# Delta u stored in 32-row half units, and the step size finished in its PSUM bank

## The chip, the cores and the metric

The kernel runs on one core of a Trainium2 chip. The metric is the device time of one launch in microseconds (us). The engines of the core are named as in the profile: PE (TensorE, matrix products), PEld (its weight loads), DVE (VectorE), ACT (ScalarE), POOL (GpSimd) and SP (SyncE, which here only issues transfers). A name with a q, such as SPq or ACTq, is an instruction by which a queue issues a transfer. Each engine takes its instructions in a fixed order.

## The reference, cut to what matters

The program is a network of four layers on 4 images of 96 channels and 64 x 64 pixels (4096 positions). Layer 0 is a selective state-space scan over four directions, layer 1 a deformable convolution with gathers, layer 2 a Fourier mixer with a feed-forward part, layer 3 a linear attention with a feed-forward part. The change touches layer 0 alone. Its core, for each of 4 images and 4 directions, with 192 channels and 16 states per channel:

```python
delta = jax.nn.softplus(dts + delta_bias[None, :, :, None])
...
def step(h, inp):
    d_t, u_t, b_t, c_t = inp
    dA = jnp.exp(d_t[..., None] * A)
    h = dA * h + (d_t * u_t)[..., None] * b_t[:, :, None, :]
    y = jnp.einsum('bkdn,bkn->bkd', h, c_t)
    return (h, y)
h0 = jnp.zeros(u.shape[:3] + (A.shape[-1],), u.dtype)
_, ys = lax.scan(step, h0, (dl, ul, bl, cl))
```

So there is a step size delta (softplus of a projection) per channel and position, a product delta times u, a decay exp(delta A) per channel and state, and the recurrence along the 4096 positions.

## The kernel before, in words

**The scan.** A unit is 8 channels by 16 states, which fill the 128 partitions, over 1024 positions. There are 4 images x 4 directions x 4 stretches of positions x 24 groups of 8 channels, 1536 units. A block is the 64 channels of one stretch, 8 units: `i` from 0 to 3 and `q` from 0 to 1. For each unit:

- `fetch` (L907, L911) has ACT's queue load the step sizes of 8 channels, each repeated for 16 states, into `da`, five units ahead. `fetch_block` (L926) has SP's queue load delta u for a block in two transfers, six units ahead. `fetch_step` (L918) loads B and C for a stretch.
- `decay` (L932): ACT takes the exponential of `da`.
- `inflow` (L938): two PE matmuls spread delta u over the 128 partitions into `db`, a PSUM tile of two banks with two buffers. Delta u is kept as three bf16 pieces whose sum is the fp32 value, so the 96 rows of the operand are 3 pieces x 32 channels, and the 0/1 matrix `rep` picks the unit's 8 channels and adds the pieces.
- `enter` (L952): DVE multiplies `db` by B in place. `recur` (L960): DVE scans.
- `weigh` (L967, L969): POOL saves the last state and multiplies by C. `total` (L983, L988): PE sums over the states into `py`. `settle` (L999) copies it out on ACT, `store` (L1006) writes it on SP's queue.

**The step sizes.** `before(b)` prepares image b: normalisation, convolution, projections, and then `steps`, one chain for each of 8 chunks of 512 positions and 6 groups of rows (4 of 128 channels of one direction, 2 of 64 channels of two directions): 192 chains. A chain is: PE projects into a PSUM bank `pd` (L769); ACT makes abs, exp, ln(1 + e) into `lw` and 1 + e into `w1` (L771 to L775); DVE corrects `w1` (L778); POOL corrects `lw` (L780); DVE adds max(pd, 0) into `rl` (L782), the step size; DVE multiplies it by u into `ex` (L785 where u is read transposed, L791 otherwise); SP stores `rl` (L794). Then ACT and PE split `ex` into the three bf16 pieces `du` (L798 to L808), and SP stores those (L812). `lw` and `w1` have one buffer, `rl` and `du` two, `ex` three.

**The order of the work.** The scan's units are laid down in order, and between them a planner lays down steps of two other streams: `ends` (the preparation of images 0 to 3, then layers 2 and 3 of each image) and `middle` (the output part of layer 0, `behind`, and layer 1, in series for each image). Each step states its cost on each engine, the PSUM banks that it holds (three are shared by these streams), and the buffers that it takes and frees. The planner keeps a clock for each engine and lays down a step where that leaves room. The program's order on each engine is the order of laying down. A step can only begin if its first engine would not idle for it, so a step that starts on ACT is laid down when ACT's planned end has passed the step's ready time. What is not laid down when the last unit is reached follows after the scan, alone.

**Waits.** An instruction waits for semaphores. The tile framework adds these waits by itself[...]. [...]

Of the kernel before, what the change touches and what calls it, by code (L numbers as in the profile page):

```python
# [10 lines left out]
BF16 = mybir.dt.bfloat16  # L11
# [9 lines left out]
L = H * W  # L21
# [23 lines left out]
def prepare(x, **w):  # L45
# [51 lines left out]
    dtp[64 : 64 + R + 1, 2:] = dtw[2:].transpose(2, 0, 1)  # L97
    a["dtw"] = dtp

    al = w["L0_conv_A_logs"].reshape(KG, DI // D8, D8, NS)  # L100
    a["al"] = c(al.transpose(3, 2, 0, 1).reshape(128, KG * DI // D8))

    ds = w["L0_conv_Ds"].reshape(KG, NG, 64).transpose(2, 1, 0)
    a["ds"] = c(np.concatenate([ds, ds]))
# [22 lines left out]
    for n in (2, 3):  # L127
# [14 lines left out]
    a["cen_c"] = wide(cen[128:], 256)  # L142

    p = np.arange(128)
    rep = (p[:, None, None] % 32 == 8 * np.arange(4)[None, :, None] + p[None, None] % 8).astype(f)
    a["rep"] = c(rep)
    a["fold"] = c(
        (p[:, None, None] % 8 + 8 * np.arange(4)[None, :, None] == np.arange(32)[None, None]).astype(f)
    )
    yy, xx = np.divmod(np.arange(L).reshape(32, 128).T, W)  # L150
    ki, kj = np.divmod(np.arange(9), 3)
# [368 lines left out]
class Unit:  # L520


    def __init__(self, b, k, step, g, i, q):
        self.b, self.k, self.step, self.g, self.i = b, k, step, g, i
        self.s = i + 4 * q
        self.back = k >= 2
        self.j = NT - 1 - step if self.back else step
        self.n = 8 * g + self.s
        self.key = f"{b}_{k}_{self.j}_{g}_{self.s}"
        self.first_of_block = i == 0 and q == 0  # L530
        self.first_of_step = self.first_of_block and g == 0
        self.ts = slice(self.j * T, (self.j + 1) * T)
        self.bc = self.du = None
# [5 lines left out]
class Layer0:  # L539
# [7 lines left out]
    def __init__(self, ctx, net, x1):  # L547
        self.net, self.x1 = net, x1
        tc, nc, ins = net.tc, net.nc, net.ins
        wp = ctx.enter_context(tc.tile_pool(name="l0w", bufs=1))  # L550
        for name in ("fold", "al", "ds"):
            setattr(self, name, net.load(name, wp))

        nc.scalar.activation(self.al, self.al, AF.Exp)
        nc.vector.tensor_scalar_mul(self.al, self.al, -1.0)

        dsum = wp.tile([128, NG], F32, name="dsum")
        nc.vector.reduce_sum(dsum, self.ds, axis=mybir.AxisListType.X)
        self.skip = wp.tile([128, NG, 128], F32, name="skip")
        for g in range(NG):  # L560
            nc.vector.tensor_scalar_mul(self.skip[:, g, :], net.ident, dsum[:, g : g + 1])

        self.wc_d = net.dram.tile([C, 9, 256], F32, name="wc_d")
        self.rep = wp.tile([128, 4, 128], BF16, name="rep16")
        self.minus = wp.tile([128, 128], BF16, name="minus")
        nc.vector.tensor_scalar_mul(self.minus, net.ident, -1.0)
        with tc.tile_pool(name="l0prep", bufs=1) as tp:
            nc.vector.tensor_copy(self.rep, net.load("rep", tp))
            w_in = net.load("w_in", tp)
            cw = tp.tile([C, 9, 256], F32, name="cwr")  # L570
            nc.sync.dma_start(cw, ins["cw"].partition_broadcast(C))
            nc.vector.tensor_mul(cw, cw, w_in[:, :256].unsqueeze(1).to_broadcast([C, 9, 256]))
            nc.sync.dma_start(self.wc_d, cw)
        dram = net.dram
        self.u_d = [dram.tile([DI, L], F32, name=f"u{b}") for b in range(B)]
        self.z_d = [dram.tile([DI, L], F32, name=f"z{b}") for b in range(B)]
        self.de_d = [dram.tile([KG, DI, L], F32, name=f"de{b}") for b in range(B)]
        self.du_d = [dram.tile([KG, 3, DI, L], BF16, name=f"du{b}") for b in range(B)]
        self.bc_d = [dram.tile([KG, 2 * NS, L], F32, name=f"bcd{b}") for b in range(B)]
        self.y_d = [dram.tile([KG, DI, L], F32, name=f"y{b}") for b in range(B)]  # L580
        self.sp = ctx.enter_context(tc.tile_pool(name="l0s", bufs=2))
        self.banks = ctx.enter_context(ExitStack())
        self.ps = self.banks.enter_context(tc.tile_pool(name="l0q", bufs=1, space=PSUM))


        self.ready, self.summed = set(), set()

        self.scanned = (0.0, 0.0)

        self.settled = 0.0  # L590
# [160 lines left out]
    def steps(self, b, ks, j, us, dtw, sm, xdbl):  # L751

        net = self.net
        nc = net.nc
        cs = slice(j * CH, (j + 1) * CH)
        tk = f"{b}_{j}_" + "".join(str(k) for k in ks)
        both = len(ks) == 2

        def tile_of(name, bufs):
            return sm.tile([128, CH], F32, name=f"{name}{tk}", tag=name, bufs=bufs)  # L760

        yield wait(new=True, takes="ex lw")


        pd = net.mm(f"pd{tk}")
        for k in ks:
            q = k % 2
            o, m = (pd[64 * q : 64 * q + 64], slice(128, DI)) if both else (pd, slice(0, 128))
            nc.tensor.matmul(o, lhsT=dtw[:, k, m], rhs=xdbl[q, j], start=True, stop=True)  # L769
        ex = tile_of("ex", 3)  # L770
        nc.scalar.activation(ex, pd, AF.Abs)  # L771
        nc.scalar.activation(ex, ex, AF.Exp, scale=-1.0)
        lw, w1 = tile_of("lw", 1), tile_of("w1", 1)
        nc.scalar.activation(lw, ex, AF.Ln, bias=net.one)
        nc.scalar.activation(w1, ex, AF.Identity, bias=net.one)  # L775
        yield cost(pe=2.2 if both else 1.1, act=2.7, holds=1, takes="rl")
        rl = tile_of("rl", 2)
        nc.vector.scalar_tensor_tensor(w1, w1, -1.0, ex, ALU.add, ALU.subtract)  # L778
        yield cost(dve=0.7, holds=1)
        nc.gpsimd.tensor_sub(lw, lw, w1)  # L780
        yield cost(pool=1.3, holds=1)
        nc.vector.scalar_tensor_tensor(rl, pd, 0.0, lw, ALU.max, ALU.add)  # L782
        yield cost(dve=0.7, frees="lw")
        if not both and ks[0] % 2:
            nc.vector.tensor_mul(  # L785
                ex.rearrange("p (w h) -> p w h", h=H),
                rl.rearrange("p (w h) -> p w h", h=H),
                us[1][:, j * NR : (j + 1) * NR, :],
            )
        else:  # L790
            nc.vector.tensor_mul(ex, rl, us[2 if both else 0][:, cs])  # L791
        parts = ((0, 64, ks[0], 128), (64, 128, ks[1], 128)) if both else ((0, 128, ks[0], 0),)
        for p0, p1, k, c0 in parts:
            nc.sync.dma_start(self.de_d[b][k][c0 : c0 + p1 - p0, cs], rl[p0:p1])  # L794
        yield cost(dve=0.7, takes="du", frees="rl")

        du = sm.tile([128, 3, CH], BF16, name=f"du{tk}", tag="du", bufs=2)
        nc.scalar.copy(du[:, 0, :], ex)  # L798
        yield cost(act=0.6, new=True)
        pr = net.mm(f"pr{tk}")  # L800
        nc.tensor.matmul(pr, lhsT=net.ident, rhs=ex, start=True, stop=False)  # L801
        nc.tensor.matmul(pr, lhsT=self.minus, rhs=du[:, 0, :], start=False, stop=True)
        nc.scalar.copy(du[:, 1, :], pr)
        yield cost(pe=1.5, act=0.6, holds=1, frees="ex")
        nc.tensor.matmul(
            pr, lhsT=self.minus, rhs=du[:, 1, :], start=False, stop=True, skip_group_check=True
        )
        nc.scalar.copy(du[:, 2, :], pr)  # L808
        yield cost(pe=0.4, act=0.6)
        for p0, p1, k, c0 in parts:  # L810
            dst = self.du_d[b][k][:, c0 : c0 + p1 - p0, cs]
            nc.sync.dma_start(dst.rearrange("s c t -> c s t"), du[p0:p1])  # L812
        self.ready.update((b, k, both, j) for k in ks)
        yield wait(frees="du")

# [66 lines left out]
    def fetch(self, u, before):  # L882
# [24 lines left out]
                nc.scalar.dma_start(add[64 * h : 64 * h + 64], src[c0 : c0 + 64, halves[h]])  # L907
        self.net.clock.add(ACT, 0.6, self.scanned[1])
        u.da = sp.tile([128, T], F32, name=f"da{u.key}", tag="da", bufs=6)
        src = self.de_d[b][k][c0 + D8 * u.s : c0 + D8 * u.s + D8, ts]  # L910
        nc.scalar.dma_start(u.da, src.unsqueeze(0).to_broadcast([NS, D8, T]))  # L911

    def fetch_step(self, u):
# [5 lines left out]

    def fetch_block(self, u):  # L920

        u.du = []
        for q in range(2):
            t = self.sp.tile([96, T], BF16, name=f"du{u.key}_{q}", tag=f"du{q}")
            c0 = 64 * u.g + 32 * q
            self.net.nc.sync.dma_start(t, self.du_d[u.b][u.k][:, c0 : c0 + 32, u.ts])  # L926
            u.du.append(t)

    def decay(self, u):
        u.decayed = self.net.clock.add(ACT, 1.15, 0.0)  # L930
# [1 line left out]
        self.net.nc.scalar.activation(u.da, u.da, AF.Exp, scale=self.al[:, a : a + 1])  # L932

    def inflow(self, u):
        u.spread = self.net.clock.add(PE, 0.8, self.scanned[1])
        db = self.ps.tile([128, 2, CH], F32, name=f"db{u.key}", tag="db", bufs=2)
        for h in range(2):
            self.net.nc.tensor.matmul(  # L938
                db[:, h, :],
                lhsT=self.rep[:96, u.s % 4, :],  # L940
                rhs=u.du[u.s // 4][:, h * CH : (h + 1) * CH],
                start=True,
                stop=True,
            )
# [847 lines left out]
```

## Time and profile before

| what | value |
|---|---|
| median of 3 runs | 8837.66 us (8813.62 to 8846.13) |
| profiled execution, its own time | 8879.74 us |
| its span | 8877.9 us |
| DVE busy | 6807.1 us (77%) |
| PE busy | 6652.4 us (75%) |
| POOL busy | 5620.9 us (63%) |
| ACT busy | 4943.6 us (56%) |
| granted TensorE clock, mean | 0.805 |

A line of a group reads: line of the kernel, engine, operation, result<-operands by the program's names, shapes, count | busy time in us, mean time of one in ns | idle time of the engine just before these, and what ended most of it. A line of a wait reads: who <- for what: us in total, times, longest. In a timeline: start, duration, engine, line, operation, and in brackets the idle time ahead of it and what ended it. The 40 digits of a row of section 2 are busy tenths of 40 equal slices of the span.

### The profile page before, as it was taken

What the parts mean: (1) busy time and instruction counts of PE and PEld (TensorE: products, weight loads), DVE (VectorE), ACT (ScalarE), POOL (GpSimd) and SP (SyncE); (2) the same over time, 40 slices, a digit from 0 to 9 for tenths busy, and PEclk for the clock granted to TensorE, in tenths of its full rate; (3) what the DMA queues carried; (4) which work ended last, traced back from release to release, by engine and by line L of the source; (5) the groups of instructions that cost most, each with busy time, mean ns of one, the idle gap of its engine ahead of it and who ended that gap; (6) DMA issues with size and microseconds to landing.
All of it is one profiled execution on the core that took longest, in us unless ns stands there. A gap on an engine that the chain in (4) does not pass through costs nothing.

```text
span 8877.9 us, 96298 instructions
## 1 busy us (share of the span) xinstructions
PE 6652.4 (75%) x31960; PEld 2922.8 (33%) x31960; DVE 6807.1 (77%) x5091; ACT 4943.6 (56%) x9062; POOL 5620.9 (63%) x4307
## 2 busy tenths in 40 slices
PE   6665967687767778777667888776778877787797
PEld 2111311122122224311222455222445532265383
DVE  0488889987888988788898887788878888636514
ACT  3564656555556768745566666445656774423323
POOL 0365656665668888666588888566887886447400
PEclk8786977788778779877777888787888887788797
DMA  1476777767678888876788988676888987444310
GB/s 48 134 201 178 187 186 223 202 176 184 190 204 228 234 225 231 212 181 187 200 226 223 230 223 225 152 181 173 212 228 211 234 204 170 108 128 146 96 55 11
DMA packets 775989, 1608.40 MB, mean 181 GB/s; under 512 B 247809, under 2 KB 339357, under 8 KB 773382
## 3 DMA queue, kind: packets, MB, share of 16 engines
q10 hardware_dynamic: 244224, 843.17, 37.0%
q1 hardware_dynamic: 457542, 532.51, 22.2%
q0 software_dynamic: 73728, 226.57, 9.7%
q8 instruction: 256, 4.19, 0.2%
q14 instruction: 239, 1.96, 0.1%
HBM read 1345.62 MB, written 256.29 MB: 180 GB/s over the span
## 4 chain that ended last, share of the span: by engine, by line
PE 35%; DVE 28%; DMA 16%; ACT 8%; issue 8%; POOL 3%; SPq 2%; ACTq 1%; DVEq 0%; another core or an unknown queue 0%; POOLq 0%
DVE hh L960 14%; DVE db L952 7%; DMA du<-du 6%; PE pc L691 4%; PE py L988 4%; PE f L1428 3%; PE db L938 3%; PE ps L1334 3%; DMA da<-de 2%; ACT g L1313 2%; PE pd L1350 2%; POOL hh L969 1%; ACT da L932 1%; PE h L1469 1%; PE py L983 1%
## 5 line engine op out<-in xcount | busy, mean ns | idle before, releaser
L969 POOL TENSOR_TENSOR hh<-hh,bc 128x1024 f32<-128x1024 f32 x1536 | 3659.8, 2385 | 346.0 <-DVE hh L960 233.6
L960 DVE TENSOR_TENSOR_SCAN hh<-da,st,db 128x1024 f32<-128x1024 f32 x1152 | 2701.0, 2345 | 236.2 <-PE py L988 98.9
L952 DVE TENSOR_TENSOR db<-db,bc 128x1024 f32<-128x1024 f32 x1536 | 1863.3, 1213 | 557.5 <-PE db L938 551.6
L932 ACT ACTIVATE da<-da,w_al 128x1024 f32<-128x1024 f32 x1536 | 1741.8, 1146 | 648.2 <-DMA da<-de 295.3
L938 PE MATMUL db<-du,rep 96*128 96x512 bf16 x3072 | 1105.0, 448 | 810.8 <-DVE hh L960 748.9
L1301 POOL DMA_INDIRECT g<-table,idx x1152 | 1210.6, 1051 | 407.2 <-issue 176.0
L988 PE MATMUL py<-hh,w_fold 128*32 128x512 f32 x6144 | 1055.6, 762 | 26.6 <-POOL hh L969 8.8
L1313 ACT ACTIVATE g<-g,wt 128x96 f32<-128x96 f32 x3456 | 963.9, 364 | 167.6 <-DMA du<-du 52.2
L960 DVE TENSOR_TENSOR_SCAN hh<-da,db 128x1024 f32<-128x1024 f32 x384 | 877.1, 2284 | 68.9 <-PE py L988 22.8
L938 PEld LDWEIGHTS <-rep 96*128 96x128 bf16 x3072 | 284.5, 107 | 1764.0 <-issue 1126.3
L1334 PE MATMUL ps<-w_ident,g 128*96 128x128 f32 x3744 | 675.3, 320 | 215.0 <-ACT g L1313 138.0
L780 POOL TENSOR_TENSOR lw<-lw,w 128x512 f32<-128x512 f32 x192 | 244.2, 1272 | 825.5 <-DVE w L778 815.6
L967 POOL COPY st<-hh 128x1 f32<-128x1 f32 x1152 | 232.4, 202 | 725.3 <-DVE hh L960 682.0
L1334 PEld LDWEIGHTS ps<-w_ident,g 128*96 128x96 f32 x3744 | 480.1, 141 | 569.4 <-ACT g L1313 249.6
L691 PE MATMUL pc<-pad,wc 96*128 96x512 f32 x1152 | 547.8, 615 | 53.4 <-DMA wc<-wc_d 46.3
L1342 ACT COPY st<-ps 96x384 f32<-96x384 f32 x384 | 179.7, 472 | 458.2 <-PE ps L1334 350.6
L801 PE MATMUL pr<-ex,w_ident 128*128 128x512 f32 x384 | 281.0, 822 | 170.0 <-DVE ex L791 87.7
L778 DVE SCALAR_TENSOR_TENSOR w<-w,ex 128x512 f32<-128x512 f32 x192 | 155.1, 808 | 289.8 <-ACT w L775 289.7
L691 PEld LDWEIGHTS pc<-pad,wc 96*128 96x128 f32 x1152 | 216.5, 195 | 336.4 <-issue 305.1
L988 PEld LDWEIGHTS py<-hh,w_fold 128*32 128x32 f32 x6144 | 155.1, 123 | 516.8 <-issue 393.8
L769 PE MATMUL pd<-xd,w_dtw 103*64 103x512 f32 (+1 forms) x512 | 268.0, 802 | 65.8 <-DVE rl L782 26.1
L1350 PE MATMUL pd<-st,wdc 96*128 96x256 f32 x1152 | 302.4, 411 | 7.8 <-ACT st L1342 4.1
(250 smaller groups left out, 8807.7 us busy)
## 6 DMA issues: line engine op xcount, KB each, us to landing
da<-de ACTq DMA_DIRECT2D x1536, 512.0 KB
du<-du SPq DMA_DIRECT2D x512, 192.0 KB
bc<-bcd SPq DMA_DIRECT2D x128, 512.0 KB
du<-du SPq DMA_DIRECT2D x128, 384.0 KB
y<-yb SPq DMA_DIRECT2D x384, 128.0 KB
de<-rl SPq DMA_DIRECT2D x128, 256.0 KB
m<-in_dft SPq DMA_DIRECT2D x128, 256.0 KB
ad<-y ACTq DMA_DIRECT2D x192, 128.0 KB
```

The lines of the kernel that those rows point to most:

```text
L691: nc.tensor.matmul(pp, lhsT=wc[:, q, g * 128 : (g + 1) * 128], rhs=pad[:, r0 + dy : r0 + dy + NR, dx : dx + W], start=(q == 0), stop=(q == 8),
L801: nc.tensor.matmul(pr, lhsT=net.ident, rhs=ex, start=True, stop=False)
L932: self.net.nc.scalar.activation(u.da, u.da, AF.Exp, scale=self.al[:, a : a + 1])
L938: self.net.nc.tensor.matmul(db[:, h, :], lhsT=self.rep[:96, u.s % 4, :], rhs=u.du[u.s // 4][:, h * CH : (h + 1) * CH], start=True, stop=True,)
L952: self.net.nc.vector.tensor_mul(u.db, u.db, u.bc[:, 0, :])
L960: nc.vector.tensor_tensor_scan(u.along(u.hh), u.along(u.da), u.along(u.db), first, ALU.mult, ALU.add)
L969: self.net.nc.gpsimd.tensor_mul(u.hh, u.hh, u.bc[:, 1, :])
L988: nc.tensor.matmul(py[p0 : p0 + 32], lhsT=self.fold[:, u.i, :], rhs=hc[:, h * CH : (h + 1) * CH], start=u.sums["add"] is None and u.i == 0 ...
L1301: nc.gpsimd.indirect_dma_start(out=g[:, k, :], out_offset=None, in_=self.tables[b % 2], in_offset=bass.IndirectOffsetOnAxis(ap=idx[:, n : ...
L1313: nc.scalar.activation(pixel, pixel, AF.Identity, scale=wt[:, n, c : c + 1])
L1334: nc.tensor.matmul(pt[:, k, :], lhsT=g[:, k, c * C : (c + 1) * C], rhs=net.ident, is_transpose=True, start=(c == 0), stop=(c == corners - 1),)
L1350: nc.tensor.matmul(po, lhsT=wdc[:, k, :], rhs=st[:, k, :], start=(k == 0), stop=(k == 8))
```

## The change

Two things change in layer 0.

The first concerns the step size. DVE no longer writes it to `rl` in SBUF but back into its PSUM bank `pd`. ACT then copies `pd` to `rl`, from where it is stored, and DVE multiplies `pd` by u. `pd` is held for one step more, and `rl` is taken later.

The second concerns delta u. In DRAM it is laid out in blocks of 32 channels and 512 positions, each with its 96 rows (3 pieces x 32 channels) together, so a chain stores it in four transfers of 32 partitions, and a block is fetched in four transfers of 24 partitions with four rows each: channel 4p + i of a 32-group sits in partition p, place i. One tile holds two halves of positions (h) and two groups of 32 channels (q) at partitions 64q + 32h. The spread matmul of half h then contracts 24 rows at that partition in place of 96, as a tile of 32 rows of the array, and `rep` is one 128 x 128 matrix. A unit now takes channels i, i + 4, i + 8, ... of its 32, so `al`, `fold` and the rows of the `da` load follow. The cost that `inflow` states to the planner goes from 0.8 to 0.5.

```diff
-    rep = (p[:, None, None] % 32 == 8 * np.arange(4)[None, :, None] + p[None, None] % 8).astype(f)
-    a["rep"] = c(rep)
+    a["rep"] = c((p[:, None] % 8 == p[None] % 8).astype(f))
...
-        self.du_d = [dram.tile([KG, 3, DI, L], BF16, name=f"du{b}") for b in range(B)]
+        self.du_d = [dram.tile([KG, NCH, DI // 32, 3 * 32, CH], BF16, name=f"du{b}") for b in range(B)]
...
         yield cost(pe=2.2 if both else 1.1, act=2.7, holds=1, takes="rl")
-        rl = tile_of("rl", 2)
...
-        nc.vector.scalar_tensor_tensor(rl, pd, 0.0, lw, ALU.max, ALU.add)
-        yield cost(dve=0.7, frees="lw")
+        nc.vector.scalar_tensor_tensor(pd, pd, 0.0, lw, ALU.max, ALU.add)
+        yield cost(dve=0.7, holds=1, frees="lw")
+        rl = tile_of("rl", 2)
+        nc.scalar.copy(rl, pd)
...
-            nc.vector.tensor_mul(ex, rl, us[2 if both else 0][:, cs])
+            nc.vector.tensor_mul(ex, pd, us[2 if both else 0][:, cs])
+        yield cost(dve=0.7, act=0.6)
         parts = ((0, 64, ks[0], 128), (64, 128, ks[1], 128)) if both else ((0, 128, ks[0], 0),)
         for p0, p1, k, c0 in parts:
             nc.sync.dma_start(self.de_d[b][k][c0 : c0 + p1 - p0, cs], rl[p0:p1])
-        yield cost(dve=0.7, takes="du", frees="rl")
+        yield wait(takes="du", frees="rl")
...
         for p0, p1, k, c0 in parts:
-            dst = self.du_d[b][k][:, c0 : c0 + p1 - p0, cs]
-            nc.sync.dma_start(dst.rearrange("s c t -> c s t"), du[p0:p1])
+            for p in range(p0, p1, 32):
+                dst = self.du_d[b][k, j, (c0 + p - p0) // 32].rearrange("(s c) t -> c s t", s=3)
+                nc.sync.dma_start(dst, du[p : p + 32])
...
-        src = self.de_d[b][k][c0 + D8 * u.s : c0 + D8 * u.s + D8, ts]
+        src = self.de_d[b][k][c0 + 32 * u.q + u.i : c0 + 32 * u.q + 32 : 4, ts]
...
-        u.du = []
+        u.du = self.sp.tile([128, 4, CH], BF16, name=f"du{u.key}", tag="du")
         for q in range(2):
-            t = self.sp.tile([96, T], BF16, name=f"du{u.key}_{q}", tag=f"du{q}")
-            c0 = 64 * u.g + 32 * q
-            self.net.nc.sync.dma_start(t, self.du_d[u.b][u.k][:, c0 : c0 + 32, u.ts])
-            u.du.append(t)
+            for h in range(2):
+                p0 = 64 * q + 32 * h
+                src = self.du_d[u.b][u.k, 2 * u.j + h, 2 * u.g + q]
+                self.net.nc.sync.dma_start(u.du[p0 : p0 + 24], src.rearrange("(p i) t -> p i t", i=4))
...
-        u.spread = self.net.clock.add(PE, 0.8, self.scanned[1])
+        u.spread = self.net.clock.add(PE, 0.5, self.scanned[1])
...
-                lhsT=self.rep[:96, u.s % 4, :],
-                rhs=u.du[u.s // 4][:, h * CH : (h + 1) * CH],
+                lhsT=self.rep[64 * u.q + 32 * h : 64 * u.q + 32 * h + 24],
+                rhs=u.du[64 * u.q + 32 * h : 64 * u.q + 32 * h + 24, u.i, :],
```

More of the change, by code (lines that the diff above doesn't have):

```diff
@@ L98, in prepare @@
     a["dtw"] = dtp
-    al = w["L0_conv_A_logs"].reshape(KG, DI // D8, D8, NS)
-    a["al"] = c(al.transpose(3, 2, 0, 1).reshape(128, KG * DI // D8))
+    al = w["L0_conv_A_logs"].reshape(KG, DI // 32, D8, 4, NS)
+    a["al"] = c(al.transpose(4, 2, 0, 1, 3).reshape(128, KG * DI // D8))
     ds = w["L0_conv_Ds"].reshape(KG, NG, 64).transpose(2, 1, 0)
@@ L144, in prepare @@
     p = np.arange(128)
-    rep = (p[:, None, None] % 32 == 8 * np.arange(4)[None, :, None] + p[None, None] % 8).astype(f)
-    a["rep"] = c(rep)
+    a["rep"] = c((p[:, None] % 8 == p[None] % 8).astype(f))
     a["fold"] = c(
-        (p[:, None, None] % 8 + 8 * np.arange(4)[None, :, None] == np.arange(32)[None, None]).astype(f)
+        (4 * (p[:, None, None] % 8) + np.arange(4)[None, :, None] == np.arange(32)[None, None]).astype(f)
     )
@@ L524, in __init__ @@
         self.b, self.k, self.step, self.g, self.i = b, k, step, g, i
+        self.q = q
         self.s = i + 4 * q
@@ L563, in __init__ @@
         self.wc_d = net.dram.tile([C, 9, 256], F32, name="wc_d")
-        self.rep = wp.tile([128, 4, 128], BF16, name="rep16")
+        self.rep = wp.tile([128, 128], BF16, name="rep16")
         self.minus = wp.tile([128, 128], BF16, name="minus")
@@ L786, in steps @@
                 ex.rearrange("p (w h) -> p w h", h=H),
-                rl.rearrange("p (w h) -> p w h", h=H),
+                pd.rearrange("p (w h) -> p w h", h=H),
                 us[1][:, j * NR : (j + 1) * NR, :],
```

## The prediction

> **What bounds the kernel now.** I first read the page: span, and the sliced rows of section 2.
>
> ```profile
> span 8877.9 us, 96298 instructions
> ...
> DVE  0488889987888988788898887788878888636514
> ```
>
> VectorE (DVE) is full from the second to the 34th slice and thin after: the scan, then a tail. Next come three windows cut at the first scan (359) and the last (7670).
>
> ```profile
> 0.00:359.00 359.00, 216.86 (x452) 84.52 (x453) 39.87 (x70) 155.83 (x193) 14.83 (x19) 0.81 0.23 67
> 359.00:7670.00 7311.00, 5487.97 (x24592) 2183.32 (x24591) 6242.09 (x4241) 4441.81 (x8179) 5229.06 (x3975) 0.80 0.78 202
> 7670.00:8878.00 1208.00, 947.58 (x6916) 655.00 (x6916) 525.14 (x782) 345.92 (x690) 377.03 (x313) 0.82 0.31 87
> ```
>
> The columns are PE, PE weight load, DVE, ACT and POOL busy. In the scan, DVE works 6242 of 7311 us, PE 75%, ACT 61%, so what DVE saves or waits there counts nearly whole. The groups by shape say what it does, and the waits of that window what it waits for.
>
> ```profile
> L960 DVE TENSOR_TENSOR_SCAN hh<-da,st,db 128x1024 f32<-128x1024 f32 x1152 | 2701.0, 2345 | 236.2 <-PE py L988 98.9 <-ACT da L932 19.9 <-DVE db L952 4.6
> L952 DVE TENSOR_TENSOR db<-db,bc 128x1024 f32<-128x1024 f32 x1536 | 1863.3, 1213 | 557.5 <-PE db L938 551.6 <-PE lnc L471 2.2 <-DMA da<-de 1.5
> L774 ACT ACTIVATE lw<-ex,one 128x512 f32<-128x512 f32 x192 | 138.6, 722 | 93.7 <-DVE rl L782 84.2 <-DVE db L952 1.2 <-ACT ex L772 0.4
> ```
>
> ```profile
> DVE db L952 <- PE db L938: 551.6, 230, 20.3
> DVE hh L960 <- PE py L988: 121.7, 89, 14.8
> DVE w L778 <- ACT w L775: 50.8, 48, 6.4
> ```
>
> A unit costs 2.33 + 1.21 us on DVE, and its largest wait (230 times) is for the spread matmuls of L938. ACT's L774 already waits for DVE's L782: it writes `lw`, which has one buffer and which L782 reads. That line matters below. Then the durations (min/median/max) of the multiply by u:
>
> ```profile
> L785 DVE TENSOR_TENSOR ex<-rl,xa x60: 1027/1076/8809, 401.2 to 4667.6; 128x512 f32<-128x512 f32 x60
> ...
> L791 DVE TENSOR_TENSOR ex<-rl,xa x62: 676/692/5358, 373.6 to 4755.8; 128x512 f32<-128x512 f32 x62
> L791 DVE TENSOR_TENSOR ex<-rl,xc x61: 677/692/3519, 364.3 to 4689.7; 128x512 f32<-128x512 f32 x61
> ```
>
> The maxima are far above the medians; the page's means are 1724 (L785), 1176 and 1010 ns (L791). Last, a timeline around a long ACT stall, and two groups of the tail.
>
> ```profile
> 5183.76 1.58 SPq L926 DMA_DIRECT2D du<-du  x2
> ...
> 5212.75 0.52 ACTq L911 DMA_DIRECT2D da<-de  x1
> 5213.32 0.91 ACT L1313 ACTIVATE g<-g,wt 128x96 f32<-128x96 f32 x3 [10.90 <-DMA du<-du]
> ```
>
> ```profile
> L1107 DVE TENSOR_TENSOR xr<-po,xr x8: 660/661/689, 7432.4 to 7739.8; 96x512 f32<-96x512 f32 x8
> ...
> L1320 DVE TENSOR_TENSOR g<-g,wt x96: 1332/1351/1360, 7866.5 to 8364.1; 128x1152 f32<-128x1152 f32 x96
> ```
>
> ACT stands 10.9 us because its da load can't be issued before a du load that SP issued 28 us earlier has landed. In the built program SP's and ACT's transfers take eight completion semaphores in turn, and each waits for the one eight before it.
>
> [...] L785 and L791 read two, L952 reads one and stays within 1195 to 1292 ns. [...] no run here shows row tiles yet.
>
> **Part 1: step size in PSUM.** L782 now writes into its bank `pd`; ACT copies it to `rl` (new L786), and DVE multiplies `pd` by u. In the built order all 192 multiplies wait for exactly that copy, and in 159 places the multiply is DVE's next instruction after L782's. So DVE stands until ACT's in-order queue reaches the copy. Between the two the emission order puts ACT work of the *next* chain: in 126 of 192 places the Ln into `lw`, which by the wait above can't start before L782 ends. Queued behind it: L775's w1 (706 ns), in 76 of the 126 the last cast of `du` (L808, 576), then the copy (an equal PSUM copy, L999: 572). With 0.06 us for each change of engine (L803 to L805):
> - 71 adjacent, with Ln and cast: 0.72 + 0.71 + 0.58 + 0.57 + 0.12 = 2.7 us, 192 us
> - 35 adjacent, with Ln: 2.1 us, 74 us
> - 34 adjacent, copy alone: 0.7 us, 24 us; 19 with the cast: 1.0 us, 19 us
> - 33 with DVE work between: 0.5 us (estimate), 17 us
>
> That is 326 us. While DVE stands, PE catches up, and some of the 0.36 us per unit lost to L938 vanishes with it: about 40. I take **+290** (ends: 192 x 0.7 = 130 if ACT always runs ahead of its Ln; 500 if the cast's matmul is late too). All who wait for scans (POOL's 234 us, PE's 749) wait longer by it.
>
> The multiply then has one SBUF input and should keep its median: 64 x (1.72 - 1.06) + 128 x (1.09 - 0.69) = **-94** (0 to -100). 192 copies load ACT by 110 us; it idles 2870 us in the scan, so 0. `pd` keeps its bank for one more step, of three.
>
> **Part 2: 32-row groups.** A pair of L938 took 0.59 us (timeline at 3001.57) with one at 0.38: the second adds 0.21; at the low clock (634 ns) about 0.43. If both row tiles run at once, that is saved each unit, of a wait that is often PE stuck behind other streams. 230 waits x 0.32 = 74, and some 50 of backlog: **-120** ([...] -350 if two thirds of 551 go).
>
> Transfers: bytes are equal, but SP issues 4 instead of 1 or 2 per write and 4 instead of 2 per fetch: 512 + 384 = 896 more beside 4376. Eight semaphores then last 2.3 units instead of 2.6 between a da load and its predecessor; those within one unit rise from 378 to 499 of 1536. ACT waits some 0.2 ms for du transfers now. Say 120 more short blocks of 2 us on ACT, a third reaching DVE: **+80** (0 to 250). `rl` is freed by the same transfers; L782 waited 5.7 us for them, now the copy does. Strided da rows are as large as before: 0. [...] at 96 KB a piece I count nothing.
>
> **Part 3: what the planner moves.** With other costs and a bank held longer, side work falls back. In the built order, before: all of image 2's gathers and 6 of the last image's 8 output chunks stand ahead of the last scan. After: 45 gathers (15 groups) and all 8 chunks stand behind it, in one stream in series, and the last layers follow. Alone the tail does 96 groups in 498 us (7866.5 to 8364.1), 15 take 78; a pair of chunks takes 37 us from its POOL add (7703) to 7740, with its load about 40, three more pairs 120. Of these 198 I take **+190** (80 to 280). The scan is relieved of about 40 us of DVE work: **-40**. Head: five multiplies at 2 us, **+10**.
>
> **Sum.** 290 - 94 - 120 + 80 + 190 - 40 + 10 = +316 us. The profiled execution took 8879.74 us (span 8877.9 plus 1.8), so 9196; it stands 42 us above the median of the runs, 8837.66, to which I add: 9154, taken as 9150.
>
> **Rivals.** *Near balance*: stalls fall where DVE would have waited for PE anyway, +130, and the tail's extra costs 80: 130 - 94 - 120 + 40 + 80 - 40 = 0 to +60, 8840 to 8900. For it: 551 us of waits to hide in. Against: the Ln's place behind L782 is fixed. *PE packing wins (faster)*: L938's pair is what is late; if row tiles take 350 of the 551 us, the stall stays at 130 to 200 and the tail at 100, then about -130: 8700. It decides once the saving exceeds 440 with my other terms, or 250 with the low ones. Against: the longest waits (20.3 us) are no matmul's length. *Semaphores bite*: each burst of four write and four fetch transfers uses up all eight, and ACT, PE and DVE stall together as at 5202: +250 instead of 80 and late copies: 9400 to 9500. *The change doesn't do what it says*: row tiles run one after another; loses the 120, 9270.
>
> **Chances.** Main, with serial row tiles: 0.62, own range 8980 to 9330. Near balance 0.16, faster 0.10, semaphores 0.12. To leave out no more than 2 in 10 the range goes to 8860 and 9430. A change of 0.5% (44 us) is about what a measurement can tell: faster 0.10, within 0.07 (half of near balance), slower 0.83.
>
> **What would show it.** Right: the multiply waits for ACT's new copy, some 200 to 400 us in the scan; its mean falls to near 0.69 and 1.06; L938's pair near 0.4 us; DVE's wait for it near 430; scan window near 7430, tail near 1400. Wrong if that wait is under 150 us, if waits for `db` fall below 250, or if the tail stays at 1208.

## The result, and the profile after

The changed kernel takes 9117.26 us (median of 4 runs, 9112.59 to 9118.69) against 8841.9 us for the kernel before in the same comparison: ratio 1.0321, 95% interval 1.0298 to 1.0345. The forecast was 9150. Chips differ a little (the kernel before took 8826 to 8895 us beside the experiments), so kernels are compared below by their ratios to the kernel before; 0.01 of it is 88.4 us.

The page of the changed kernel, its span and DVE's row of slices:

```profile
span 9110.6 us, 96986 instructions
...
DVE  0478976797768887866789899888889999327613
```

The first third was nearly all 8 and 9 and now has 6 and 7 among them: it is where the step sizes of the images are made. The windows cut at the first and last scan (columns as before: PE, PEld, DVE, ACT and POOL busy, clock, DMA share, GB/s):

```profile
0.00:355.00 355.00, 219.00 (x453) 84.35 (x454) 39.79 (x70) 160.46 (x202) 14.11 (x19) 0.80 0.23 67
355.00:7740.00 7385.00, 5341.94 (x24198) 2076.64 (x24196) 6090.99 (x4208) 4432.81 (x8072) 5099.38 (x3899) 0.76 0.78 198
7740.00:9111.00 1371.00, 1068.29 (x7166) 713.22 (x7166) 593.67 (x885) 390.28 (x773) 463.54 (x384) 0.80 0.34 92
```

The scan took 74 us longer although DVE has 151 us less to do in it; the tail took 163 us longer and holds 103 more DVE instructions and 71 more on POOL. The granted clock in the scan fell from 0.80 to 0.76, which no step of the forecast had. DVE's waits in the scan window:

```profile
DVE db L957 <- PE db L943: 377.5, 183, 17.7
DVE ex L794 <- ACT rl L786: 344.7, 110, 7.8
DVE ex L788 <- ACT rl L786: 154.6, 53, 17.9
DVE hh L965 <- PE py L993: 86.1, 81, 6.2
```

Two rows are new: the multiply waits for the copy, 163 times in the scan, 499 us. The wait for `db` fell by 174. The groups by shape (busy us, mean ns, idle us ahead and what ended it):

```profile
L965 DVE TENSOR_TENSOR_SCAN hh<-da,st,db 128x1024 f32<-128x1024 f32 x1152 | 2701.3, 2345 | 195.7 <-PE py L993 67.4 <-POOL ya L1057 8.3 <-ACT da L937 8.2
L957 DVE TENSOR_TENSOR db<-db,bc 128x1024 f32<-128x1024 f32 x1536 | 1861.6, 1212 | 379.1 <-PE db L943 377.5
```

A scan and its multiply take what they took. The multiply by u, by its line's durations (min/median/max):

```profile
L788 DVE TENSOR_TENSOR ex<-pd,xa x64: 996/1031/1073, 281.9 to 4384.3; 128x512 f32<-128x512 f32 x64
```

Its maximum is now 4% above its median; before it was eight times the median (8809 against 1076). A timeline of one wait of the usual length (start, duration, engine, line, in brackets the idle time ahead):

```profile
1369.62 0.68 DVE L783 SCALAR_TENSOR_TENSOR pd<-pd,lw 128x512 f32<-128x512 f32 x1
...
1370.07 0.60 ACT L773 ACTIVATE ex<-pd 128x512 f32<-128x512 f32 x1 [1.12 <-PE pd L771]
...
1370.70 0.63 ACT L774 ACTIVATE ex<-ex 128x512 f32<-128x512 f32 x1
...
1371.37 0.72 ACT L776 ACTIVATE lw<-ex,one 128x512 f32<-128x512 f32 x1
...
1371.99 0.71 ACT L777 ACTIVATE w<-ex,one 128x512 f32<-128x512 f32 x1
1372.60 0.56 ACT L812 CAST du<-pr 128x512 bf16<-128x512 f32 x1
1373.07 0.59 ACT L786 COPY rl<-pd 128x512 f32<-128x512 f32 x1
...
1373.69 0.69 DVE L794 TENSOR_TENSOR ex<-pd,xc 128x512 f32<-128x512 f32 x1 [3.39 <-ACT rl L786]
```

DVE's L783 is done at 1370.30. ACT has just started the next chain, late because PE was; its four activations and a cast stand ahead of the copy, and DVE stands 3.39 us. In the tail, the multiply by the gather weights:

```profile
L1325 DVE TENSOR_TENSOR g<-g,wt x112: 1337/1357/1430, 7745.5 to 8631.7; 128x1152 f32<-128x1152 f32 x112
```

112 of these instead of 96: 16 groups of image 2 now stand behind the last scan. Last, PE's groups of the spread matmuls and of the sums over the states, in the kernel before and in the changed one:

```profile
L938 PE MATMUL db<-du,rep 96*128 96x512 bf16 x3072 | 1105.0, 448 | 810.8 <-DVE hh L960 748.9 <-DMA du<-du 39.2 <-ACT g L1313 7.1
L988 PE MATMUL py<-hh,w_fold 128*32 128x512 f32 x6144 | 1055.6, 762 | 26.6 <-POOL hh L969 8.8 <-ACT yb L999 8.8 <-issue 6.4
```

```profile
L943 PE MATMUL db<-du,rep 24*128 24x512 bf16 x3072 | 710.3, 462 | 1070.9 <-DVE hh L965 1043.8
...
L993 PE MATMUL py<-hh,w_fold 128*32 128x512 f32 x6144 | 1113.9, 801 | 43.6 <-ACT yb L1004 20.6
```

Busy time counts overlap once: 710.3 / 1536 is 0.46 us per pair, where the kernel before had 1105.0 / 1536 = 0.72. So two row tiles do overlap. But a matmul of `py`, which the change doesn't touch, went from 762 to 801 ns.

### The profile page after: what moved, and what is told of

It is laid out like the page before. It is cut to its first block, busy times and chain, and to the rows that moved or that the text cites. A ratio compares the mean times of both kernels' runs of the same rounds, so it can differ in the third digit from the quotient of the medians.

```text
span 9110.6 us, 96986 instructions
## 1 busy us (share of the span) xinstructions
PE 6629.2 (73%) x31816; PEld 2874.2 (32%) x31816; DVE 6724.4 (74%) x5161; ACT 4983.6 (55%) x9046; POOL 5577.0 (61%) x4301
## 4 chain that ended last, share of the span: by engine, by line
PE 19%; DVE 14%; DMA 6%; issue 4%; ACT 4%; POOL 2%; SPq 1%; ACTq 1%; DVEq 0%; POOLq 0%
DVE hh L965 7%; DVE db L957 4%; PE f L1433 3%; PE ps L1339 2%; PE py L993 2%; DMA da<-de 2%; PE pd L1355 2%; ACT g L1318 2%; POOL hh L974 1%; PE db L943 1%; PE h L1474 1%; PE yp L1513 1%; PE zp L1499 1%; ACT da L937 1%; PE py L988 1%
## 5 line engine op out<-in xcount | busy, mean ns | idle before, releaser
L974 POOL TENSOR_TENSOR hh<-hh,bc 128x1024 f32<-128x1024 f32 x1536 | 3635.4, 2369 | 349.1 <-DVE hh L965 229.8
L943 PE MATMUL db<-du,rep 24*128 24x512 bf16 x3072 | 710.3, 462 | 1070.9 <-DVE hh L965 1043.8
L993 PE MATMUL py<-hh,w_fold 128*32 128x512 f32 x6144 | 1113.9, 801 | 43.6 <-ACT yb L1004 20.6
L1318 ACT ACTIVATE g<-g,wt 128x96 f32<-128x96 f32 x3264 | 909.9, 364 | 165.3 <-DVE hh L965 57.0
L943 PEld LDWEIGHTS <-rep 24*128 24x128 bf16 x3072 | 159.7, 93 | 2127.6 <-issue 1331.8
L805 PE MATMUL pr<-ex,w_ident 128*128 128x512 f32 x384 | 331.2, 958 | 307.0 <-DVE ex L794 148.5
L771 PE MATMUL pd<-xd,w_dtw 103*64 103x512 f32 (+1 forms) x512 | 311.1, 915 | 48.5 <-DMA w_dtw<-in_dtw 19.1
L1355 PE MATMUL pd<-st,wdc 96*128 96x256 f32 x1152 | 323.9, 433 | 5.4 <-ACT du L812 3.0
L1442 ACT COPY d<-f 128x512 f32<-128x512 f32 x192 | 112.1, 584 | 362.7 <-PE f L1433 362.2
```

The lines of the kernel that those rows point to most:

```text
L943: self.net.nc.tensor.matmul(db[:, h, :], lhsT=self.rep[64 * u.q + 32 * h : 64 * u.q + 32 * h + 24], rhs=u.du[64 * u.q + 32 * h : 64 * u.q ...
L974: self.net.nc.gpsimd.tensor_mul(u.hh, u.hh, u.bc[:, 1, :])
L993: nc.tensor.matmul(py[p0 : p0 + 32], lhsT=self.fold[:, u.i, :], rhs=hc[:, h * CH : (h + 1) * CH], start=u.sums["add"] is None and u.i == 0 ...
L1318: nc.scalar.activation(pixel, pixel, AF.Identity, scale=wt[:, n, c : c + 1])
L1355: nc.tensor.matmul(po, lhsT=wdc[:, k, :], rhs=st[:, k, :], start=(k == 0), stop=(k == 8))
```

## The experiments

The theory at the start was that of the forecast: the wait for the copy and what the planner moves cost the time, row tiles win some back. Twelve kernels take the change apart. All ratios are to the kernel before:

| kernel | groups | step size in PSUM | price of the spread | ratio (95%) | scan / tail, us | clock |
|---|---|---|---|---|---|---|
| before | no | no | 0.8 | 1 | 7310 / 1208 | 0.805 |
| changed | yes | yes | 0.5 | 1.0321 (1.0298 to 1.0345) | 7384 / 1371 | 0.765 |
| e1 | yes | no | 0.5 | 0.9942 (0.9929 to 0.9954) | 7317 / 1115 | 0.776 |
| e2 | no | yes | 0.8 | 1.0314 (1.0268 to 1.0360) | 7425 / 1275 | 0.803 |
| e3 | yes | multiply first | 0.5 | 1.0212 (1.0167 to 1.0257) | 7275 / 1371 | 0.763 |
| e4 | yes | multiply first, copy a step | 0.5 | 0.9936 (0.9915 to 0.9958) | 7215 / 1211 | 0.776 |
| e5 | no | no | 0.5 | 1.0053 (1.0032 to 1.0073) | 7418 / 1110 | 0.812 |
| e6 | transfers only | no | 0.8 | 1.0061 (1.0042 to 1.0080) | 7368 / 1185 | 0.803 |
| e7 | yes | yes, two `lw` | 0.5 | 1.0258 (1.0228 to 1.0289) | 7367 / 1354 | 0.762 |
| e8 | yes | yes | 0.8 | 1.0175 (1.0142 to 1.0207) | 7372 / 1301 | 0.763 |
| e9 | yes | no | 0.8 | 0.9851 (0.9821 to 0.9882) | 7171 / 1247 | 0.776 |
| e10 | yes | multiply first, copy a step | 0.8 | 0.9908 (0.9879 to 0.9937) | 7134 / 1305 | 0.779 |
| e11 | no | multiply first, copy a step | 0.8 | 1.0065 (1.0033 to 1.0096) | 7249 / 1324 | 0.808 |
| e12 | yes, no row tiles | no | 0.8 | 0.9775 (0.9739 to 0.9811) | 7119 / 1229 | 0.814 |

"Scan" is from the first scan to the end of the last, "tail" what follows, and the clock is the mean of the span, all in the profiled execution. The price is what `inflow` tells the planner.

### The two halves apart

e1 has the groups with the price of 0.5, and the step size as before:

```diff
+        rl = tile_of("rl", 2)
...
-        nc.vector.scalar_tensor_tensor(pd, pd, 0.0, lw, ALU.max, ALU.add)
-        yield cost(dve=0.7, holds=1, frees="lw")
-        rl = tile_of("rl", 2)
-        nc.scalar.copy(rl, pd)
+        nc.vector.scalar_tensor_tensor(rl, pd, 0.0, lw, ALU.max, ALU.add)
+        yield cost(dve=0.7, frees="lw")
...
-            nc.vector.tensor_mul(ex, pd, us[2 if both else 0][:, cs])
-        yield cost(dve=0.7, act=0.6)
+            nc.vector.tensor_mul(ex, rl, us[2 if both else 0][:, cs])
...
```

> The 32-row groups alone; the step size is made in SBUF as before. Copy theory (the time is lost where VectorE waits for ScalarE's copy, and in the tail): no copy, no such wait; the spread pair falls to about 0.46 us, VectorE's wait for it from 552 to about 400 us, the tail stays near 1200 us: 8700 us (8640 to 8780). Transfer theory (896 more transfers and their semaphores make the loss): slower than before, 8900 us or more, with more ScalarE idle time that ends on a transfer than 701 us.

e2 has the step size in PSUM alone, units and price as before (the diff of the change's first part, nothing else).

> The step size in PSUM alone; delta u and the planner's cost as before. Copy theory: about 500 us of VectorE waits for the copy, 94 us back from the multiply, some 60 us of other waits hidden, a tail longer by about 130 us (all 8 output chunks of the last image stand behind the scan, no gathers of image 2): 9280 us (9180 to 9350), slower than the whole change. Transfer theory: the copy is hidden in waits for PE, 8900 us or less.

e1 came out at 8773.22 us and e2 at 9083.83 (before: 8826.06). The signs are as expected: the step size costs, with 492 us of waits for the copy in its scan, and the groups gain. e1 lies in its range; e2 lies some 100 us below its own (9180 to 9350), although the waits are of the length expected. And e1's wait for `db` did not fall (558 us), its scan took as long as before, and the whole gain sat in a shorter tail. It looked as if the planner's price had won it and the matmuls nothing. The part about the price fell with e5; the part about the matmuls is taken up in e12.

### The multiply ahead of the copy

e3 swaps the two readers of `pd` in the changed kernel, so that the multiply doesn't wait for ACT. e4 also makes the copy a step of its own for the planner:

```diff
-        rl = tile_of("rl", 2)
-        nc.scalar.copy(rl, pd)
...
             nc.vector.tensor_mul(ex, pd, us[2 if both else 0][:, cs])
+        yield cost(dve=0.7, holds=1)
+        rl = tile_of("rl", 2)
+        nc.scalar.copy(rl, pd)
-        yield cost(dve=0.7, act=0.6)
+        yield cost(act=0.6)
```

That is e4. In e3 the first added line is absent and the last pair is as in the changed kernel.

> The whole change with two statements exchanged: VectorE's multiply is laid down before ScalarE's copy, all else in the same order. Copy theory: the multiply no longer waits, ScalarE waits for the multiply in its place; about 500 us of VectorE waits go, some 50 to 100 come back because ScalarE is held up; the tail stays at 1370 us: 8700 us (8620 to 8800). Rival (VectorE's stall only hides waits for PE, so they come back): the wait for the spread matmuls rises by several hundred us and the time stays above 9000 us.

> As the exchange, and the copy is a step of its own, so that the planner lays it down when ScalarE has room. In program order the scan is followed by 2 chunks of the last image and no gathers of image 2. Copy theory with the tail as its second part: as the exchange with a tail near 1200 us, 8550 us (8450 to 8680). If the tail is not made by what stands behind the scan, it stays near 1370 us and the time near that of the exchange.

e3: 9004.84 us, e4: 8769.94. Both lie above their ranges (8620 to 8800 and 8450 to 8680); for e3 the rival was right, the waits came back. DVE's waits in the scan of e3:

```profile
DVE db L957 <- PE db L943: 516.7, 234, 17.0
DVE w L779 <- ACT w L777: 189.9, 124, 5.6
```

The 499 us are gone, and other waits grew: `db` by 139, and `w` from 20 to 190, since ACT's copy now stands waiting for the multiply with the next chain behind it. Taking the copy's wait away in an unchanged order is worth 1.0321 - 1.0212, 96 us, a fifth of its length. That is a lower bound of what the stall cost, since the waits for `w` belong to the exchange. The tail kept its 1371 us. Giving the copy its own step in addition is worth 244 more: the order changes, the tail falls to 1211 and the scan by 60. The copy's stated 0.6 us of ACT in the multiply's step makes that step begin on ACT for the planner, so it is laid down when ACT's planned end allows; that this is how the order came to be so much worse is argued from the planner's rule, the time is shown.

### The price, the transfers, and what the copy queues behind

e5 changes one number of the kernel before, e8 sets it back in the changed kernel:

```diff
-        u.spread = self.net.clock.add(PE, 0.8, self.scanned[1])
+        u.spread = self.net.clock.add(PE, 0.5, self.scanned[1])
```

> The kernel before with the planner's price of L938 alone set to 0.5 (no groups, no change to the step size). In its built order 753 DVE instructions follow the last scan, as in the kernel with the groups alone, instead of 784. Theory 1, the groups won their 0.6% only by the price (order of the side work): tail about 1115 us, scan as before, granted clock about 0.80, time 8750 to 8790. Rival, the row tiles themselves won it: tail near 1208 us, time 8830.

> The changed kernel with the planner's price of L943 set back to 0.8; all else as changed. If the price decides what falls behind the last scan: no gathers of image 2 there (288 in place of 334 side instructions of that kind), tail about 1275 us as with the step size alone, time about 9020 to 9050. Rival, the tail is due to the change itself: tail near 1371, time 9110.

e5: 8885.96 us, above both forecasts. The tail did fall by 98 us, as in e1, but the scan grew by 107: the price alone loses 0.5%. So it had not won e1's time; against e5, the groups are worth 1.1%, all of it in the scan, and the shorter tail is the price's. My reading of e1 compared it with a kernel laid down in another order. e8: 9007.75 us, tail 1301 instead of 1371, near the first of its two forecasts. In the changed kernel the price costs 1.0321 - 1.0175, 129 us.

e6 gives the kernel before the change's number of transfers (896 more), whole rows of 1 KB:

```diff
-            nc.sync.dma_start(dst.rearrange("s c t -> c s t"), du[p0:p1])
+            for p in range(p0, p1, 32):
+                part = dst[:, p - p0 : p - p0 + 32]
+                nc.sync.dma_start(part.rearrange("s c t -> c s t"), du[p : p + 32])
...
-            self.net.nc.sync.dma_start(t, self.du_d[u.b][u.k][:, c0 : c0 + 32, u.ts])
+            for h in range(2):
+                hs = slice(u.j * T + h * CH, u.j * T + (h + 1) * CH)
+                src = self.du_d[u.b][u.k][:, c0 : c0 + 32, hs]
+                self.net.nc.sync.dma_start(t[:, h * CH : (h + 1) * CH], src)
```

> The kernel before with delta u stored and fetched in the change's numbers (896 more transfers of the same bytes), whole units, same order, no row tiles. Theory of the prediction: more waits for completion semaphores, ACT idle on transfers in the scan up from 701 us by 100 to 250, time up by 80: 8900. Rival, as the comparison of the traces has it: nothing or less, ACT idle on transfers 400 to 700 us, 8800 to 8840.

e6: 8882.41 us, 54 more than before; ACT's idle time on transfers in the scan was 718 us against 701. The number of transfers costs something, but not through ACT as the forecast had it.

e7 gives `lw` two buffers (`tile_of("lw", 2)`) in the changed kernel.

> The changed kernel with two buffers for lw, so that ACT's Ln of the next chain no longer stands behind DVE's L783 ahead of the copy; same order. If the Ln is what the copy queues behind, DVE's wait for the copy falls from 509 us to 100 to 250; the time falls by less, 30 to 110 us (9010 to 9080), since the exchange of the two readers, which took the wait away, won 112; the tail stays near 1371. Rival, the copy is late for another reason (the last cast, or the change of engines): wait above 400, time 9100.

e7: 9073.74 us. The wait for the copy stayed (482 us), so the theory of the Ln falls. The kernel is still 1.0321 - 1.0258, 56 us, faster than the changed one; the waits for the copy and for `w` are 17 us shorter each, and where the rest came from is open. DVE's waits in its scan:

```profile
DVE ex L794 <- ACT rl L786: 341.6, 109, 10.7
DVE ex L788 <- ACT rl L786: 140.2, 53, 17.9
```

In the changed kernel the Ln had stood behind DVE's L783 for 62 us in 41 places only. The copy is late as the timeline shows: ACT runs late behind PE, and the whole next chain, four activations and often a cast, is ahead in its queue, whether its Ln may start or not.

### Groups and price taken apart, then the row tiles

e9 is the groups with the price of 0.8. It has the order of e6, and of the kernel before, on every engine. e10 is e4 with that price, e11 the same without groups.

> The 32-row groups alone, with the planner's price of L938 left at 0.8: on every engine in the order of the kernel with the added transfers (e6), from which it differs only in that the two spread matmuls sit on 24-row tiles. If the row tiles themselves bring what e1 less e5 shows (-113 us) and the price only costs time: about 8720, 0.982 of e6, granted clock about 0.77 where e6 has 0.803, tail near 1185. Rival, tiles and price only work together (e1 alone is faster than before because its side work is laid down otherwise): near e6, 8830 to 8880.

> The changed kernel with the exchange of e4 (multiply before the copy, the copy a step of its own) and the price at 0.8. If the price costs here what it costs the changed kernel (110 us less at 0.8): 8660, the fastest so far, wait for the copy 0, tail near 1180. Rival, the price acts only through what falls behind the last scan, which here is no gather at either price: 8770 as e4.

> The step size in its PSUM bank with the exchange of e4, no groups, price 0.8. If the copy's wait and its place were all that made the step size in PSUM slow, this is at or below the kernel before, since the contention (94 us) is gone: 8740 to 8800, granted clock about 0.80, multiply means near 0.69 and 1.06. Rival, the bank held longer costs by itself: 8900 or more.

e9: 8757.6 us, 0.9851 of before, 2.1% below e6; its wait for `db` is 439 us in the whole run against 571. This is the kernel of the change's second part alone, and it is faster. e10: 8800.56 us, no better than e9, and e11 is slower than before (1.0065): with the wait for the copy gone and the long multiplies too (DVE's busy time in e10's scan is 6133 us, in e9's 6257), the scan of e10 gains 38 us and its tail loses 58, since 855 DVE instructions follow the last scan in place of 783. Both expectations for e10 and e11 were too hopeful.

Four pairs of kernels have the same order on DVE, ACT and POOL and differ in the groups alone: the kernel before and e9 (-132 us), e2 and e8 (-123), e11 and e10 (-139), e5 and e1 (-98). So the groups as a whole win some 100 to 140 us beside whatever else is changed.

Was it the row tiles that made e9 fast? e12 keeps e9's blocks in DRAM, its transfers and its order, but puts the four pieces of a block on 96 adjacent partitions and lets each spread matmul take all 96 rows, with a 0/1 matrix that is zero outside its 24:

```diff
-                p0 = 64 * q + 32 * h
+                p0 = 48 * q + 24 * h
...
-                lhsT=self.rep[64 * u.q + 32 * h : 64 * u.q + 32 * h + 24],
-                rhs=u.du[64 * u.q + 32 * h : 64 * u.q + 32 * h + 24, u.i, :],
+                lhsT=self.rep[:96, 2 * u.q + h, :],
+                rhs=u.du[:96, u.i, :],
```

> The groups alone with price 0.8 (as e9: same blocks of 32 channels in DRAM, same transfers of 24 partitions, same order), but the four pieces of a block lie on 96 adjacent partitions and the spread matmul takes all 96 rows with a 0/1 matrix that is zero outside its 24, so that no two matmuls run on row tiles. If the row tiles on PE won e9 its time: as e6, about 1.003 to 1.008 of the kernel before, 8850 to 8900, pair of matmuls about 0.72 us of PE, waits for db about 570, granted clock about 0.80. Rival, the layout in DRAM (fetches of whole rows of 4 KB in place of 1 KB pieces, ACT idle on transfers down from 718 to 408 us) won it: near 0.985, granted clock about 0.80 as well.

e12: 8691.76 us, ratio 0.9775, the fastest of all: 2.2% faster than the kernel before, and 0.8% faster than e9. The row tiles did not win the time (without them, 8850 to 8900 us had been expected if they had); they cost some. PE's groups of e9 and then of e12:

```profile
L991 PE MATMUL py<-hh,w_fold 128*32 128x512 f32 x6144 | 1125.5, 807 | 26.9 <-POOL hh L972 9.8 <-ACT yb L1002 9.3 <-issue 7.7
L941 PE MATMUL db<-du,rep 24*128 24x512 bf16 x3072 | 705.9, 457 | 892.6 <-DVE hh L963 843.8 <-DMA du<-du 23.4 <-issue 11.8
```

```profile
L943 PE MATMUL db<-du,rep 96*128 96x512 bf16 x3072 | 1102.5, 447 | 850.6 <-DVE hh L965 781.1 <-DMA du<-du 37.1 <-issue 9.2
L993 PE MATMUL py<-hh,w_fold 128*32 128x512 f32 x6144 | 1058.7, 764 | 25.0 <-ACT yb L1004 10.4 <-POOL hh L974 6.6 <-issue 5.6
```

The pairs save 397 us of PE time, but the mean clock is 0.776 with row tiles and 0.814 without, and the other matmuls take longer: `py` alone 67 us more. PE is busy 5419 us in e9's scan and 5427 in e12's: 8 us are left of the saving. DVE waits for `db` as long in both, in e9:

```profile
DVE db L955 <- PE db L941: 438.8, 202, 20.7
```

and in e12:

```profile
DVE db L957 <- PE db L943: 434.7, 204, 22.1
```

What did win is what e12 and e9 have and e6 has not: the layout. A block's fetches read whole stretches of DRAM, 4 KB to a partition, in place of 1 KB pieces. The queue of SP shows it. First the fetches of e6 by their line (min/median/max in ns):

```profile
L931 SPq DMA_DIRECT2D du<-du x768: 680/732/12532, 343.5 to 7632.7; - x192
```

A wait of its SP queue (us in total, times, longest):

```profile
SPq L1011 <- DMA du<-du: 384.0, 61, 22.6
```

The fetches of e12:

```profile
L932 SPq DMA_DIRECT2D du<-du x768: 289/362/11352, 339.6 to 7383.7; - x192
```

And the same wait of its SP queue:

```profile
SPq L1011 <- DMA du<-du: 187.3, 41, 10.7
```

Issuing one fetch takes SP half the time (362 against 732 ns; 747 before, with half as many), and the store of y waits half as long for fetches of delta u to land. ACT's idle time on transfers in the scan is 411 us, against 718 in e6, and DVE's wait for `db` in the whole run 435 against 571. Bytes are the same. But a fetch lands in more parts. The pages count packets, of e6 and then of e12:

```profile
DMA packets 822206, 1608.51 MB, mean 180 GB/s; under 512 B 257153, under 2 KB 422429, under 8 KB 819590
DMA packets 773822, 1608.54 MB, mean 185 GB/s; under 512 B 264065, under 2 KB 355613, under 8 KB 771206
```

With the same stores and the same number of fetches, e12 has 6912 more packets under 512 B (e9 as well), 9 for each of the 768 fetches. A fetch also lands in 9 parts more, counted by the updates of its semaphore after its issue: where their record is whole, 3 in the kernel before (344 of 384 fetches) and in e6, 12 in the changed kernel (761 of 768), e9 and e12. How many DMA engines brought a piece was not shown. The median time from issue to landing is 8.2 us in e6 and 6.1 in e12.

Two other things come with the layout, the channels of a unit (every fourth, so `da` loads strided rows) and one tile for a block in place of two. A `da` load is no slower for it: its issue takes a median of 522 ns in both, and it lands after 6.93 us in e6, 6.45 in e12. No run separates the longer pieces, the number of parts and the single tile, so the share of each is open.

## Why the prediction was right, and where it was not

The size was right: 316 us forecast on the profiled run, 275 measured between the medians (9117.26 - 8841.9); the ratios give 284. That the sum came so close is in good part luck: single terms are off by some 190 and 250 us, and the errors cancel. The ratios give a path from the kernel before to the changed one, each step one difference (the layout with what comes with it; the last two also lay the side work down in another order):

| step | from | to | us (0.01 = 88.4) | forecast |
|---|---|---|---|---|
| number of transfers | before | e6 | +54 | +80 |
| layout of delta u | e6 | e12 | -253 | 0 |
| row tiles | e12 | e9 | +67 | -120 |
| step size in PSUM | e9 | e8 | +286 | +290 - 94 + 10, and a part of +190 - 40 |
| price 0.5 | e8 | changed | +129 | not a term; a part of +190 - 40 |

A difference of two such ratios is known to about 40 us, so each sign stands; the steps would come out somewhat differently in another order (the price costs 47 us alone, e5, and 80 on the groups, e9 to e1; the step size in PSUM costs 278 without the groups, e2).

**Part 1, the copy's wait.** That the multiply waits for the copy, and that the step size in PSUM is the largest loss, was right. Both only read `pd`, but in the program the multiply waits for the copy, in the scan 163 times, 499 us. Three parts of the step failed. The length was mis-sized: 326 us forecast, 499 in the scan, because ACT comes to its chain late (it waits for PE) and all four activations stand ahead of the copy, where I let ACT be at the Ln; two `lw` buffers shortened it by 17 us only. The share that hides was too small: I took 40 us, but when the exchange took the 499 us away, 139 us of waits for `db` came back and only 96 us were won. The 169 us by which the wait for `w` grew are the exchange's own; counting them as well, the stall cost 96 to 265 us (an estimate), not 290. And the order of the work counts as much as the stall: the copy as a step of its own won 244 more. The rival of near balance put the stall at 130, because much of it hides, which lies in that span; it came to too low a total because it priced the tail and the order at 40.

**The long multiplies**, the contention of e11's expectation. The -94 was right to a few us: 64 x (1.724 - 1.031) + 128 x (1.090 - 0.692) = 95 us of DVE time. In the kernel before, 59 of the 192 multiplies took over 1.2 times the median of their line; 58 of the 59 ran beside POOL's L969, as did 58 of the 133 others. In the changed kernel, with one operand in PSUM, 36 ran beside POOL's multiply (L974), and none of the 192 took over 1.2 times the median: the maximum of L788 is 1073 ns where it was 8809. The traces show the two together, not the cause. The time does not follow the gain, though: e10 and e11 have it, without the copy's wait, and are 50 and 57 us slower than e9 and the kernel before, in an order of their own with longer tails.

**Part 2.** The row tiles themselves run at once: two took 0.46 us in place of 0.72, 1.56 times as fast. The step from there to -120 us failed: it valued the shorter pair at the clock of before, and the clock fell from 0.805 to 0.765. The 0 for the layout ("at 96 KB a piece I count nothing") was the larger error, 253 us, in the part of the change that I had read as bookkeeping. It was an estimate with no run behind it. The traces show a fetch landing in 3 parts before and in 12 after, four times as many. The forecast of 430 us for the wait for `db` is met in e9 (439), for another reason than the one given. The transfers' +80 was right in size (54), but ACT's waits, through which I derived it, did not grow.

**Part 3.** The tail came to 1371 us, forecast 1400, with the gathers and chunks that the built order had shown. Its cause is not the longer-held bank alone: 70 us of it go with the price (e8: 1301), and all 160 with the copy's own step at the same price (e4: 1211). I had treated the price as given with the rest; it was one number to undo.

What the run showed of the marks set: multiply means, scan window (7384, forecast 7430) and tail right; the copy's wait above its 200 to 400; `db` at 377 below its 430, since the copy's wait hid a part.

**The best version.** e12, the groups without row tiles, without the step size in PSUM and at the old price, is 0.9775 of the kernel before (0.9739 to 0.9811).

## What to carry to other kernels

A new wait costs what is left when the waits that it hides are taken off. An exchange in the same order bounds it: here taking away 499 us of waiting won 96 us. Where a planner lays out the program, hold the order fixed when parts are compared, and cost each number and each step boundary that it is told as a part of the change. And when a change to a matmul comes with a new data layout, try the layout without the matmul: here the layout won 253 us, and the row tiles lost 67 of them. When a transfer's shape changes, count in the trace in how many parts it lands, before and after.

## What was not expected of the hardware

With the spread matmuls on row tiles of 24 rows, the granted clock was 0.762 to 0.779 in all eight kernels that have them (the changed one, e1, e3, e4, e7 to e10), and 0.803 to 0.814 in the six that have not. e9 and e12 differ in nothing else on PE, and show 0.776 and 0.814; the kernel before showed 0.802 to 0.812 beside the one and 0.803 to 0.811 beside the other, so it is not the chip. The trace of the clock holds only full and half, and half takes 39% of the time in the kernel before, 47% in the changed one, 45% in e9, 37% in e12. Why row tiles lower it, no run shows.

How the rows lie in DRAM halved SP's time to issue a fetch of the same bytes: 732 ns for 96 rows of 1 KB (e6), 362 ns for 24 partitions of 4 KB (e12). A fetch also landed in 12 parts in place of 3.
